# Layer 2 of a four-layer model on one core: a buffer for every gathered pair of rows, the first half's gathers issued during the second half's routing, and GpSimd's instructions in written order

## The chip, the cores and the metric

The kernel runs on one core of a Trainium2 chip. The metric is the device time of one launch in microseconds (us). The engines are called as in the profile: PE is TensorE's matmul (PEld its weight loads), DVE is VectorE, ACT is ScalarE, POOL is GpSimd and SP is SyncE, which here only issues DMAs. POOL issues DMAs too, among them the indirect ones that gather rows by a list of indices.

## The reference

Four layers work on 4 x 512 = 2,048 tokens of 256 numbers in float32. Each layer normalizes the tokens and adds an attention part and a feed-forward part to them:

```python
xn = _layernorm(x, axis=-1)
x = x + _L2_attn_ref(xn, ...) + _L2_ffn_ref(xn, ...)
```

Layer 2 is the one that is changed. Its attention part mixes the heads inside each token:

```python
q = (x @ Wq.T + bq).reshape(b, l, h, hd)
kv = (x @ Wkv.T + bkv).reshape(b, l, 2, hd)
k, v = (kv[:, :, 0], kv[:, :, 1])
attn = jnp.einsum('blhd,bld->blh', q, k)[..., None] / math.sqrt(hd)
attn = jax.nn.softmax(attn, axis=-1)
out = (attn * v[:, :, None, :]).reshape(b, l, -1)
```

Its feed-forward part sends each token to 2 of 8 small experts, and all tokens through one shared gated unit:

```python
scores = jax.nn.softmax(jnp.einsum('th,eh->te', xf, gate_w), axis=-1)
topk_w, topk_i = jax.lax.top_k(scores, K)                 # K = 2 of E = 8
topk_w = topk_w / jnp.sum(topk_w, axis=-1, keepdims=True)
cw = jnp.zeros_like(scores).at[jnp.arange(T)[:, None], topk_i].add(topk_w)
g = jnp.einsum('th,ehi->eti', xf, wg)
u = jnp.einsum('th,ehi->eti', xf, wu)
eo = jnp.einsum('eti,eih->eth', jax.nn.silu(g) * u, wd)
y = jnp.einsum('te,eth->th', cw, eo)
shared = jax.nn.silu(xf @ sg) * (xf @ su) @ sd
return (y + shared).reshape(b, s, h)
```

## The kernel before

The 2,048 tokens lie as 16 tiles of 128 rows; the running sum x stays in on-chip memory, and xnT holds the normalized tokens turned. Layer 2 treats the tokens in two halves of 8 tiles. For each half:

- `Half.dispatch` routes: `router` (L1199) computes the scores, and the rest counts how many tokens each expert gets and gives each chosen (token, expert) pair a slot in a list sorted by expert. The list has up to 23 tiles of 128 slots, `PAIRS` groups them into 11 pairs of tiles and a last single one. The result is `ids` (L1342), which row of the normalized tokens belongs in each slot, and `expert`, which expert each tile uses.
- `Half.gather` (L1367 to L1376) fetches the rows: one indirect DMA per tile, issued by POOL, from a copy of the normalized tokens in DRAM into a buffer `xs` that holds one pair.
- `Half.experts` runs the pairs through PE in a short pipeline: `turn` transposes the gathered rows (L1390, copied by ACT at L1395), `hidden` multiplies by the gate and up weights (L1402), ACT applies Silu (L1409) and DVE multiplies (L1410), `turn_hidden` transposes that (L1416, L1418), and `down` multiplies by the down weights (L1424), which DVE copies to `os` (L1429) and SP writes to DRAM (L1431).
- `Half.combine` gathers each token's two results (L1468, POOL) and adds them to x with their weights on DVE (L152).

`head_mix` (L1148) is the attention part, one sequence of four tiles at a time: PE projects (L142), DVE adds the bias into `qkv` (L1160), DVE and ACT compute the softmax `s` (L1165 to L1176), POOL multiplies it with v (`prod`, L1177) and DVE adds that to x (L1182). `qkv` and `prod` have one buffer each.

`weave` takes several such generators and writes their pieces one after another, always from the one that is the least far along in its share. `Layer2.run` calls it three times: the shared unit with the routing of both halves; then the experts of the first half with the mixer and the gathers of the second half; then the experts of the second half with the combining of the first. The gathers of the first half are pulled by its `experts`: two pairs at the start and one in each step of its loop, into three buffers (`xs0`); the second half has twelve buffers of its own (`xs1`).

What the program writes is not yet the order of an engine's instructions. The framework draws that order when the program is complete: it models the time of each instruction and lets an engine take the earliest written one of those that are ready by the model; waits for buffers count as well. Each engine then runs its list strictly in that order. `keep_in_program_order` ties an instruction behind the one that was written before it for the same engine.

Pools of buffers are stacked from two ends of on-chip memory. A pool takes the space of earlier ones once these are closed, and its first use then waits for the last reader of what it overlaps. Layer 2's pools are opened from the right: `t_rows`, `t_xs` (the gathered rows), `t_temp` (the experts' temporaries) and `h_t` (the mixer's and the shared unit's, called the mixer's pool here).

Of the kernel before, what the change touches and what calls it, by code (L numbers as in the profile page):

```python
# [15 lines left out]
P = 128  # L16
NB, SEQ, DM = 4, 512, 256
# [65 lines left out]
def v3(ap, b):  # L83
    return ap.rearrange("p (a b) -> p a b", b=b)
# [54 lines left out]
def project_tokens(c, out, w, cols, tokens):  # L139

    for d in range(2):
        c.nc.tensor.matmul(  # L142
            out, lhsT=c.xnT[:, d, tokens], rhs=w[:, d, cols], start=(d == 0), stop=(d == 1)
        )
# [69 lines left out]
def weave(c, *streams, flush=True):  # L214

    live = [[start * total, total, gen] for gen, total, start in streams]
    while live:
        s = min(live, key=lambda s: s[0] / s[1])  # L220
        cost = next(s[2], None)
        if cost is None:
            live.remove(s)
        else:
            s[0] += cost
        c.step()
    if flush:
        c.step(True)
# [644 lines left out]
def product_key_pieces(c, a, keep, pool, dram, xn):  # L873
# [110 lines left out]
    for k in range(K):  # L984
        gather(0, k)
# [162 lines left out]
def head_mix(c, pool, w, b):  # L1148

    nc = c.nc  # L1150
    H, HD, W = 16, 16, 288
    wqkv = v3(w[:, : 2 * W], W)
    bias = w[:, 2 * W : 3 * W]
    qkv = c.tile(pool, [P, TPB, W], "qkv")
    c.settle(b)
    for t in range(TPB):
        tt = b * TPB + t
        pq = c.ps()[:, :W]
        project_tokens(c, pq, wqkv, slice(0, W), slice(tt * P, (tt + 1) * P))
        nc.vector.tensor_add(qkv[:, t, :], pq, bias)  # L1160
        yield 0.5
    full = [P, TPB, H, HD]
    prod = c.tile(pool, full, "prod")
    heads = lambda v: v.rearrange("p t (h d) -> p t h d", d=HD)
    nc.vector.tensor_mul(  # L1165
        prod, heads(qkv[:, :, :256]), qkv[:, :, 256:272][:, :, None, :].to_broadcast(full)
    )
    s = c.tile(pool, [P, TPB, H], "s", bufs=2)
    nc.vector.tensor_reduce(s, prod, AX.X, ALU.add)

    top = c.tile(pool, [P, TPB, H], "top", bufs=2)
    nc.vector.tensor_copy(top, s)
    nc.vector.tensor_sub(s, s, top)
    nc.scalar.activation(s, s, AF.Exp, scale=HD ** -0.5)
    nc.vector.reciprocal(top, s)
    nc.vector.tensor_mul(s, s, top)  # L1176
    nc.gpsimd.tensor_mul(  # L1177
        prod, s[:, :, :, None].to_broadcast(full),
        qkv[:, :, 272:288][:, :, None, :].to_broadcast(full),
    )  # L1180
    x = c.x[:, b * TPB : (b + 1) * TPB, :]
    nc.vector.tensor_add(x, x, prod.rearrange("p t h d -> p t (h d)"))  # L1182
    c.part_done(b)
    yield 1.0
# [45 lines left out]
PAIRS = [[t for t in (2 * j, 2 * j + 1) if t < NS] for j in range((NS + 1) // 2)]  # L1230
# [3 lines left out]
class Half:  # L1234
# [129 lines left out]
        nc.vector.tensor_mul(w, w, tot[:, None, :].to_broadcast([P, 2, HT]))  # L1364
        yield 1.0

    def gather(self, pool, bufs, js):  # L1367

        for j in js:
            x = self.xs[j] = self.c.tile(pool, [P, 2, DM], f"xs{self.hf}", bufs=bufs)  # L1370
            for i, t in enumerate(PAIRS[j]):
                self.c.nc.gpsimd.indirect_dma_start(
                    out=x[:, i, :], out_offset=None, in_=self.xn,
                    in_offset=bass.IndirectOffsetOnAxis(ap=self.ids[:, t : t + 1], axis=0),
                )
            yield 1.0  # L1376

    def experts(self, weights, pool, opool, more):


        c, nc = self.c, self.c.nc
        pairs, xs = PAIRS, self.xs
        xsT, hs, hT = {}, {}, {}

        def turn(j):
            pt = c.ps("tr")
            n = len(pairs[j])
            for i in range(n):
                for d in range(2):
                    nc.tensor.transpose(  # L1390
                        pt[:, (2 * i + d) * P : (2 * i + d + 1) * P],
                        xs[j][:, i, d * P : (d + 1) * P], c.ident,
                    )
            xsT[j] = c.tile(pool, [P, 4, P], "xsT", bufs=2)
            nc.scalar.copy(xsT[j][:, : 2 * n, :], v3(pt[:, : 2 * n * P], P))  # L1395

        def hidden(j):
            ph = v3(c.ps(), 2 * P)
            n = len(pairs[j])
            for i, t in enumerate(pairs[j]):  # L1400
                for d in range(2):
                    nc.tensor.matmul(  # L1402
                        ph[:, i, :], lhsT=xsT[j][:, 2 * i + d, :],
                        rhs=weights[:, bass.ds(where[t] + 2 * d * P, 2 * P)],
                        start=(d == 0), stop=(d == 1),
                    )
            sg = c.tile(pool, [P, 2, P], "gate", bufs=2)
            hs[j] = c.tile(pool, [P, 2, P], "hs", bufs=2)
            nc.scalar.activation(sg[:, :n, :], ph[:, :n, :P], AF.Silu)  # L1409
            nc.vector.tensor_mul(hs[j][:, :n, :], sg[:, :n, :], ph[:, :n, P:])  # L1410

        def turn_hidden(j):
            pt = c.ps("tr")
            n = len(pairs[j])
            for i in range(n):
                nc.tensor.transpose(pt[:, i * P : (i + 1) * P], hs[j][:, i, :], c.ident)  # L1416
            hT[j] = c.tile(pool, [P, 2, P], "hsT", bufs=2)
            nc.scalar.copy(hT[j][:, :n, :], v3(pt[:, : n * P], P))  # L1418

        def down(j):  # L1420
            po = v3(c.ps("acc"), DM)
            n = len(pairs[j])
            for i, t in enumerate(pairs[j]):
                nc.tensor.matmul(  # L1424
                    po[:, i, :], lhsT=hT[j][:, i, :],
                    rhs=weights[:, bass.ds(where[t] + 4 * P, DM)], start=True, stop=True,
                )
            os = c.tile(opool, [P, 2, DM], "os", bufs=2)
            nc.vector.tensor_copy(os[:, :n, :], po[:, :n, :])  # L1429
            rows = self.out[2 * j * P : (2 * j + n) * P, :]  # L1430
            nc.sync.dma_start(rows.rearrange("(i p) d -> p i d", p=P), os[:, :n, :])  # L1431

        where = []
        N = len(pairs)
        if more:
            next(more)
            next(more)
        for lo in (0, 12):
            where.extend(nc.values_load_multi_w_load_instructions(
                self.expert[:1, lo : min(lo + 12, NS)], engines=[mybir.EngineType.PE],  # L1440
                min_val=0, max_val=(E8 - 1) * EW,
                skip_runtime_bounds_check_because="the chip has limited them to the last expert's",
            )[1])
        turn(0)
        yield 0.5
        for j in range(N + 2):
            if more:
                next(more, None)
            if j < N:
                hidden(j)  # L1450
                yield 1.7
            if j + 1 < N:
                turn(j + 1)
            if j >= 2:
                down(j - 2)
                yield 0.9
            if 1 <= j <= N:
                turn_hidden(j - 1)
            yield 0.6
# [22 lines left out]
class Layer2:  # L1482
# [24 lines left out]
    def run(self):  # L1507
        c, a = self.c, self.a
        self.rows = self.pool("t_rows")
        with ExitStack() as stack:  # L1510
            xs, temp, mixer = (self.pool(name, stack) for name in ("t_xs", "t_temp", "h_t"))
            unit = c.unit(a["t_shared"])
            h_small = c.tile(mixer, [P, 864], "h_small")
            c.nc.sync.dma_start(h_small, a["h_unit"])

            def dispatch():
                for half in self.halves:
                    yield from half.dispatch()

            def mix():  # L1520
                for b in range(NB):
                    yield from head_mix(c, mixer, h_small, b)

            shared = glu_pieces(c, mixer, [unit], n=2, width=256, loaded=True, bufs=4)
            first, last = self.halves
            every = range(len(PAIRS))
            experts = [
                half.experts(self.weights, temp, self.rows, more)
                for half, more in ((first, first.gather(xs, 3, every)), (last, None))
            ]  # L1530
            weave(c, (shared, 41.0, 0.0), (dispatch(), 34.0, 0.0), flush=False)
            weave(
                c, (experts[0], 40.0, 0.0), (mix(), 12.0, 0.0),
                (last.gather(xs, len(PAIRS), every), 12.0, 0.0), flush=False,
            )
            weave(c, (experts[1], 40.0, 0.0), (first.combine(self.rows), 11.0, 0.2), flush=False)

# [232 lines left out]
```

## Time and profile before

| | us |
|---|---|
| runs of the kernel | 3228.06, 3241.74, 3240.93; median 3240.93 |
| profiled execution | 3211.92, of it span 3210.0 |
| PE busy | 3093.7 (96% of the span) |
| DVE busy | 1858.1 (58%) |
| ACT busy | 1262.3 (39%) |
| POOL busy | 653.1 (20%) |
| mean granted TensorE clock | 0.991 |

Layer 2 lies between about 1576 and 1755 us of the span. The 46 gathers of both halves are 46 instructions of L1372 on POOL between 1601.3 and 1686.3 us, with a median of 0.949 us each; from their issue to the landing of the rows it takes 2.7 to 7.1 us, with a median of 3.4. Layer 3 fills the time from 1755 on, with PE busy nearly throughout.

A row of a timeline gives start, duration, engine, line, operation, output and inputs, and in brackets how long the engine had been idle and what ended that. The table by stage gives busy time of each engine in a stretch; PEclk in it is the part of its full clock that PE was granted.

### The profile page before, as it was taken

How to read it: one execution, taken by the hardware profiler on the slowest of the kernel's cores; microseconds unless marked ns; L12 is line 12 of the kernel's file. 1: busy time of each engine (PE TensorE's matmuls, PEld its weight loads, DVE VectorE, ACT ScalarE, POOL GpSimd, SP SyncE). 2: the span in 40 equal slices, each digit the busy share in tenths (PEclk: the TensorE clock that was granted, in tenths of full speed). 3: DMA queues.
4: the chain of work that ended last, by engine and by line, in shares of the span. 5: the costliest groups of instructions: out<-in, count | busy, mean ns of one | idle time of the engine just before them, and what ended most of it. 6: DMA issues, size and time to landing. Idle time of an engine off the chain costs nothing.

```text
span 3210.0 us, 35838 instructions
## 1 busy us (share of the span) xinstructions
PE 3093.7 (96%) x12502; PEld 1888.0 (59%) x12502; DVE 1858.1 (58%) x4730; ACT 1262.3 (39%) x2910; POOL 653.1 (20%) x525
## 2 busy tenths in 40 slices
PE   8999999998899999999989999999999999999999
PEld 5566556565555555555567565665665665555555
DVE  4778778887677677768656655545545522222222
ACT  4434444443455666657525433333333411111111
POOL 0464546556300122322053100000000000000000
PEclk9999999999999999999999999999999999999999
DMA  3232323332311144344133000000000000000000
GB/s 122 83 107 94 122 89 105 101 96 80 98 35 35 42 118 110 97 102 136 57 102 118 15 1 27 1 27 1 7 14 1 20 20 20 20 20 20 0 0 27
DMA packets 88947, 183.59 MB, mean 57 GB/s; under 512 B 14176, under 2 KB 57200, under 8 KB 84160
## 3 DMA queue, kind: packets, MB, share of 16 engines
q1 hardware_dynamic: 74304, 133.48, 13.0%
q0 software_dynamic: 14176, 47.01, 5.9%
q8 instruction: 99, 1.62, 0.2%
q10 hardware_dynamic: 288, 0.82, 0.1%
q14 instruction: 80, 0.66, 0.1%
HBM read 159.38 MB, written 12.98 MB: 54 GB/s over the span
## 4 chain that ended last, share of the span: by engine, by line
PE 74%; DVE 12%; DMA 5%; POOL 4%; ACT 3%; issue 2%; SPq 1%; DVEq 0%; ACTq 0%; POOLq 0%
PE mm L134 28%; PE acc L203 8%; PE mm L627 8%; PE mm L142 5%; PE acc L1091 4%; PE acc L643 3%; DMA G<-own 3%; DVE cy L268 2%; DVE G L409 2%; PE tr L1083 2%; PE tr L806 2%; PE acc L850 2%; PE acc L863 2%; POOL y L458 1%; DMA psw<-pes 1%
## 5 line engine op out<-in xcount | busy, mean ns | idle before, releaser
L134 PE MATMUL mm<-xnT,wu 128*128 128x512 f32 x2128 | 958.5, 597 | 7.4 <-ACT sg L388 2.9
L134 PEld LDWEIGHTS mm<-xnT,wu 128*128 128x128 f32 x2128 | 400.4, 191 | 461.2 <-issue 432.6
L634 ACT ACTIVATE pr<-pr,nm 128x128 f32<-128x128 f32 (+3 forms) x512 | 285.9, 559 | 305.3 <-DVE nm L630 302.7
L195 ACT ACTIVATE sg<-mm 128x512 f32<-128x512 f32 x168 | 99.9, 595 | 604.8 <-PE mm L134 604.6
L196 DVE TENSOR_TENSOR hT<-sg,mm 128x512 f32<-128x512 f32 x168 | 115.1, 685 | 383.3 <-PE mm L134 372.8
L203 PE MATMUL acc<-wu,hT 128*128 128x256 f32 x1344 | 304.8, 380 | 0.6 <-DVE hT L196 0.5
L630 DVE CUSTOM_DVE_ANT_0 pr<-mm,late 128x128 f32<-128x128 f32 (+3 forms) x512 | 244.8, 483 | 83.4 <-PE mm L627 78.6
L203 PEld LDWEIGHTS acc<-wu,hT 128*128 128x128 f32 x1344 | 252.2, 190 | 53.6 <-issue 20.4
L134 PE MATMUL mm<-xnT,w_in 128*128 128x512 f32 x512 | 232.7, 598 | 7.2 <-DVE cy L268 5.1
L967 POOL DMA_INDIRECT e<-in_p_experts,ids x128 | 128.3, 1002 | 494.2 <-DVE x L152 463.2
L409 DVE TENSOR_TENSOR_SCAN G<-G,eye 128x1024 f32<-128x1024 f32 x64 | 156.7, 2448 | 55.9 <-DMA G<-own 55.8
L627 PE MATMUL mm<-kf,qf 128*128 128x128 f32 (+3 forms) x512 | 176.8, 445 | 8.9 <-DVE qf L785 6.4
L435 POOL TENSOR_TENSOR G<-G,CB 128x1024 f32<-128x1024 f32 x64 | 151.2, 2363 | 149.0 <-ACT CB L361 79.7
L627 PE MATMUL mm<-k,q 128*128 128x128 f32 (+3 forms) x512 | 176.6, 435 | 1.1 <-DVE q L1056 1.1
L268 DVE SCALAR_TENSOR_TENSOR cy<-mm,ws,cy 128x509 f32<-128x509 f32 (+2 forms) x216 | 158.5, 741 | 29.8 <-ACT cy L264 26.4
L421 ACT ACTIVATE xD<-xc,ws 128x128 f32<-128x128 f32 x256 | 84.3, 390 | 203.0 <-POOL y L458 197.1
L134 PEld LDWEIGHTS mm<-xnT,w_in 128*128 128x128 f32 x512 | 97.2, 192 | 112.4 <-issue 97.8
L152 DVE SCALAR_TENSOR_TENSOR x<-acc,cw,x 128x256 f32<-128x256 f32 x128 | 61.9, 484 | 155.6 <-PE acc L203 155.6
L1091 PE MATMUL acc<-PT,V 128*128 128x512 f32 (+3 forms) x512 | 149.5, 433 | 0.0
L151 DVE TENSOR_TENSOR x<-acc,x 128x256 f32<-128x256 f32 x176 | 74.0, 422 | 129.0 <-PE acc L643 98.3
L1056 DVE TENSOR_SCALAR q<-mm,bias 128x512 f32<-128x512 f32 x64 | 48.0, 750 | 169.1 <-PE mm L134 169.1
L495 PE MATMUL tr<-wo,y 128*128 128x256 f32 x512 | 128.8, 395 | 9.1 <-DVE x L151 3.5
(306 smaller groups left out, 4977.2 us busy)
## 6 DMA issues: line engine op xcount, KB each, us to landing
G<-own SPq DMA_DIRECT2D x64, 512.0 KB, 4.2
w_in<-in_m_units SPq DMA_DIRECT2D x16, 1024.0 KB, 5.0
eb<-since SPq DMA_DIRECT2D x96, 128.0 KB, 3.4
wu<-in_o_units SPq DMA_DIRECT2D x8, 1536.0 KB, 6.6
wo<-in_m_units SPq DMA_DIRECT2D x16, 512.0 KB, 4.2
psw<-pes SPq DMA_DIRECT2D x128, 64.0 KB, 2.5
wu<-in_f_units SPq DMA_DIRECT2D x4, 1536.0 KB, 7.1
wu<-in_l_units SPq DMA_DIRECT2D x4, 1408.0 KB, 9.6
```

The costliest lines, as they stand in the source:

```text
L134: c.nc.tensor.matmul(out, lhsT=w[:, d, cols], rhs=c.xnT[:, d, tokens], start=(d == 0), stop=(d == 1))
L142: c.nc.tensor.matmul(out, lhsT=c.xnT[:, d, tokens], rhs=w[:, d, cols], start=(d == 0), stop=(d == 1))
L203: nc.tensor.matmul(po, lhsT=hT[k][:, t * P : (t + 1) * P], rhs=wd[:, k, :], start=(i == 0), stop=(i == per - 1),)
L268: nc.vector.scalar_tensor_tensor(y[:, j:], src[:, : SEQ - j], conv[:, k, 3 - j : 4 - j], y[:, j:], ALU.mult, ALU.add,)
L409: nc.vector.tensor_tensor_scan(flat, flat, eye.rearrange("p h t -> p (h t)"), 0.0, ALU.mult, ALU.add)
L435: nc.gpsimd.tensor_mul(G, G, seqs[b][2][:, t, :][:, None, :].to_broadcast([P, HG, P]))
L495: nc.tensor.matmul(po, lhsT=y[:, k, :], rhs=groups[i][1][:, k, :], start=(k == 0), stop=(k == 3))
L627: nc.tensor.matmul(sc, lhsT=q[:, i * P : n], rhs=k[:, :n], start=True, stop=True)
L630: nc.vector.tensor_tensor_reduce(out=pr, in0=sc, in1=late[:, SEQ - n :], scale=1.0, scalar=-NEG, op0=ALU.add, op1=ALU.min, accum_out=nm,)
L634: nc.scalar.activation(pr, pr, AF.Exp, bias=nm, scale=-1.0, accum_out=total)
L967: nc.gpsimd.indirect_dma_start(out=e, out_offset=None, in_=a["p_experts"], in_offset=bass.IndirectOffsetOnAxis(ap=ids[:, t, k : k + 1], ax ...
L1091: nc.tensor.matmul(z[:, j * P :], lhsT=head["V"][:, j, h, :], rhs=head["PT"][:, j, j * P :], start=(j == 0), stop=(j == TPB - 1),)
```

## The change

The change touches the gathers of layer 2, their buffers and one multiplication.

- `gather` no longer has a number of buffers and a list of pairs as arguments. Both halves use one tag, `xs`, with 24 buffers, one for each pair of both halves.
- The gathers of the first half are written between the pieces of the second half's routing, one pair a piece, instead of being pulled by the first half's `experts`; the argument `more` and its calls go.
- The gathers of both halves, and the mixer's multiplication on POOL, are tied into the order in which they are written.
- In the second weave the share of the second half's gathers is counted as 16 instead of 12.

```diff
-    nc.gpsimd.tensor_mul(
+    c.tc.keep_in_program_order(nc.gpsimd.tensor_mul(
         prod, s[:, :, :, None].to_broadcast(full),
         qkv[:, :, 272:288][:, :, None, :].to_broadcast(full),
-    )
+    ))
...
-    def gather(self, pool, bufs, js):
-
-        for j in js:
-            x = self.xs[j] = self.c.tile(pool, [P, 2, DM], f"xs{self.hf}", bufs=bufs)
-            for i, t in enumerate(PAIRS[j]):
-                self.c.nc.gpsimd.indirect_dma_start(
+    def gather(self, pool):
+
+        for j, pair in enumerate(PAIRS):
+            x = self.xs[j] = self.c.tile(pool, [P, 2, DM], "xs", bufs=2 * len(PAIRS))
+            for i, t in enumerate(pair):
+                self.c.tc.keep_in_program_order(self.c.nc.gpsimd.indirect_dma_start(
                     out=x[:, i, :], out_offset=None, in_=self.xn,
                     in_offset=bass.IndirectOffsetOnAxis(ap=self.ids[:, t : t + 1], axis=0),
-                )
+                ))
             yield 1.0
...
-    def experts(self, weights, pool, opool, more):
+    def experts(self, weights, pool, opool):
...
-        if more:
-            next(more)
-            next(more)
...
-            if more:
-                next(more, None)
...
+            first, last = self.halves
+
             def dispatch():
-                for half in self.halves:
-                    yield from half.dispatch()
+                yield from first.dispatch()
+                rows = first.gather(xs)
+                for piece in last.dispatch():
+                    next(rows, None)
+                    yield piece
+                yield from rows
...
-            first, last = self.halves
-            every = range(len(PAIRS))
-            experts = [
-                half.experts(self.weights, temp, self.rows, more)
-                for half, more in ((first, first.gather(xs, 3, every)), (last, None))
-            ]
+            experts = [half.experts(self.weights, temp, self.rows) for half in self.halves]
             weave(c, (shared, 41.0, 0.0), (dispatch(), 34.0, 0.0), flush=False)
             weave(
-                c, (experts[0], 40.0, 0.0), (mix(), 12.0, 0.0),
-                (last.gather(xs, len(PAIRS), every), 12.0, 0.0), flush=False,
+                c, (experts[0], 40.0, 0.0), (mix(), 12.0, 0.0), (last.gather(xs), 16.0, 0.0),
+                flush=False,
             )
```

## The prediction

> **What bounds the kernel now.** I read four views, from coarse to fine. The share of busy time and the busy slices come first: TensorE (PE) is busy 96% of the span, so only a stretch in which it is not busy can give time back. The table by stage of layer 2 (columns: stretch, its length, busy time and count on PE, PEld, DVE, ACT, POOL, then the granted TensorE clock, the DMA share, GB/s) finds one:
>
> ```profile
> 1591.30:1612.60 21.30, 21.27 (x104) 14.76 (x104) 11.96 (x44) 4.53 (x7) 5.79 (x6) 1.00 0.16 38
> 1615.10:1639.60 24.50, 24.10 (x105) 15.94 (x105) 15.33 (x61) 2.38 (x4) 8.87 (x10) 1.00 0.16 44
> 1639.60:1652.50 12.90, 12.64 (x61) 10.30 (x61) 6.26 (x12) 4.86 (x10) 10.16 (x10) 1.00 0.71 221
> 1652.50:1664.10 11.60, 0.03 (x1) 0.06 (x1) 0.78 (x2) 1.91 (x3) 8.62 (x10) 0.62 0.54 127
> 1664.10:1668.70 4.60, 4.60 (x12) 3.30 (x13) 1.02 (x2) 0.59 (x1) 3.62 (x4) 0.50 0.43 103
> 1668.70:1705.00 36.30, 35.95 (x182) 30.06 (x180) 23.60 (x43) 15.43 (x31) 15.96 (x12) 1.00 0.36 93
> ```
>
> For 11.6 us PE does nothing, and for the 4.6 us after that it works at half its clock. The waits of that stretch name the cause: the transposes of a gathered pair (L1390) wait for its rows.
>
> ```profile
> PE tr L1390 <- DMA xs<-xn_half,ids: 11.6, 1, 11.6
> DVE x L1182 <- POOL prod L1177: 8.3, 3, 4.1
> ```
>
> Why the rows are late stands in POOL's timeline (start, duration, engine, line, operation; idle before and its releaser in brackets):
>
> ```profile
> 1601.29 1.00 POOL L1372 DMA_INDIRECT xs<-xn_half,ids  x1 [86.14 <-DVE ids L1342]
> ...
> 1607.65 0.95 POOL L1372 DMA_INDIRECT xs<-xn_half,ids  x1 [0.30 <-issue]
> 1622.26 1.01 POOL L1372 DMA_INDIRECT xs<-xn_half,ids  x1 [13.66 <-PE tr L1390]
> 1623.58 1.00 POOL L1372 DMA_INDIRECT xs<-xn_half,ids  x1 [0.30 <-issue]
> 1630.62 0.95 POOL L1372 DMA_INDIRECT xs<-xn_half,ids  x1 [6.04 <-DVE tot L1363]
> ...
> 1660.41 0.94 POOL L1372 DMA_INDIRECT xs<-xn_half,ids  x1 [0.30 <-issue]
> ...
> 1670.13 1.95 POOL L1177 TENSOR_TENSOR prod<-s,qkv 128x1024 f32<-128x1024 f32 x1
> ```
>
> Six gathers fill the first half's three buffers. Two more follow when a buffer is read. Then, from 1630.62, when the second half's indices are there, come its 23 gathers in one run: the 24th and 25th issue from 1630.62, at 1659.15 and 1660.41, are pair 4 of the first half, and the chain of waits gives the last of them 3.53 us to land, at 1663.9. Pair 4 was needed at 1652.5. So the stall is an order on POOL, forced by three buffers.
>
> **The change, part by part.**
>
> *Buffers and the earlier gathers.* All 23 gathers of the first half can be issued from 1601.29, one every 1.25 us (0.95 of issue and 0.30 of idle): 23 x 1.254 = 28.8, so the last leaves at about 1630 and lands by 1634 (3.4 us median). The second half's indices come at 1630.34, so its gathers don't move later for it. Pair 4 lands near 1617 for a need at 1652.5. The wait of 11.6 us goes. What ends last in its place: ACT still has the Exp and its table loads, with the gate of pair 3 ending at 1654.43 and the copy of pair 4 (0.59) after that, so pair 4's first product starts at about 1655.1 where it started at 1669.07. PE fills the gap with the down product (0.86) and a mixer product (0.97). That is 14.0 us: 11.6 of wait, and of the slow stretch 2.3 (4.6 at clock 0.50 does what 2.3 at 1.00 does), with 0.1 from reading starts.
>
> The clock: the rows show 0.50 for 4.6 us after an empty 11.6. The Trainium skill (TensorE: Matmul & The Clock Gate, "What's actually happening") gives the slow time after an idle window as about 3.4 us, so an estimate by that page returns 1.7 us and not 2.3, and the sum would be 0.6 smaller; the measured row decides.
>
> *The mixer's product on GpSimd (L1177), now in written order.* In trace order it stands behind three pairs of the second half's gathers, then four, four and one pair between the others (progress 2/12, 5/12, 8/12, 11/12 of the mixer's stream against j/16 of the gathers' stream). The six gathers end near 1638; the product waits for s on DVE, ready at 1653.59; so it runs at 1653.6 and not at 1670.13. Queued behind it on POOL are the other gathers of the second half; who waits for those is the second half's experts, whose transposes start at 1706.0 now and 1692 then. Eight gathers (10.0) and one product (1.95) make 12.0 us between two products, against the 13.0 to 13.9 by which they follow each other now (1670.13, 1684.05, 1697.68, 1710.72). So gathers end before each product is due; the last row is asked for after the third product, at about 1683, and lands at 1686.5. Cost on PE: 0, hidden by that slack of 1 us or more a sequence. If the cover goes, DVE's add (L1182) waits; today it waits up to 4.1 us with PE at work. I keep 0 to 5 for the range.
>
> A rule speaks against gathering beside routing. The rows: the eight gathers issued beside routing took 0.95 to 1.01 us, with DVE busy 11.96 of 21.3; beside the mixer's wide DVE products some took up to 1.93. The Trainium skill (SBUF — State Buffer, "SBUF: two separate sides") holds that descriptor writing for a DMA from GpSimd is locked out while VectorE runs an instruction in a two-port mode, and gives 3.1 us for one of 0.62. By that, as an estimate, 23 gathers cost 23 x 2.5 = 57 us more, POOL is free only at 1687, and the kernel gets slower by tens of us; the rows of this routing show none of it, and I go by them.
>
> *More space.* The pool of rows grows from 15 to 24 tiles of 2,048 bytes, so what is opened after it (t_temp, h_t) lies 18,432 bytes lower. Today the load of h_small starts at 1580.80 and ACT's first Silu of the shared GLU waits 3.92 us, both until layer 1's last L863 ends (1580.73): the mixer's pool overlaps buffers that L863 reads. Lower down it lies in layer 1's other pool, free when L850 ends (1576.23). So that Silu can start up to 3.1 us earlier. Bounds: 0 to 3.1 gained, but DVE is busy 15.91 of 16.70 us between 1574.6 and 1591.3, so only about 0.8 of it can move, and I take 0.4. The lower mixer also reaches into layer 3's first pool: its bias load (SP, 1576.29) and mask (DVE, 0.38 and 0.21) then wait for the mixer's end, near 1700. On SP the bias load then stands between the writes of expert rows (L1431). First read: 1757.4. Cost 0, hidden by those 57 us; without them, about 3.3 (the landing of h_small's load).
>
> *Pulled pairs.* The calls by which the experts pulled gathers issue nothing else; the same 46 DMAs move the same bytes. Cost 0. Layer 3, 1,455 us with PE busy nearly throughout, keeps its instructions.
>
> **Sum:** 14.0 + 0.4 = 14.4 us less. The profiled execution took 3211.92 (span 3210.0 and 1.9 around it), so 3197.5 on its own scale. The median of the runs is 3240.93, which is 29.0 more and not explained by the trace; I carry the difference over: 3226.5.
>
> **Rivals.**
> - *More goes than the stall* (0.20). Other PE gaps of layer 2 are 1.16 (for ACT's Silu), 0.78, 0.82, 2.5 (1612.6 to 1615.1) and 1.05 us, and the order is drawn anew. For: buffers no longer hold transposes back. Against: most wait for DVE chains that stay. All of it: 6.3 more, 3220; at best.
> - *Half is taken back* (0.11). A new wait of 5 us at the first products, since pair 4 now meets the Exp's table loads (1.28 each) and the late add of the mixer: 9 gained, 3231.5. For: ACT ran the gate of pair 3 at 1654.05, after PE had already stopped. Against: the same loads at 1681.51 and 1695.14 cost PE nothing.
> - *It doesn't do what it says* (0.05): rows come early but the products stay behind something else, 3241. Against: only the rows' arrival ended that wait.
> - *Slower* (0.16): POOL becomes the pace in the mixer stage. If gathers run at the slow 1.93 + 0.30 = 2.23, the first half's end at 1652.6, six of the second at 1666.0, and the first product is 12.4 late; with 4.1 of slack, PE loses 8.3. Each of the next two products comes 8 x 2.23 + 2.0 = 19.8 after the last, against 13.8: 6.0 each. With three restarts at half clock, 2.3 each: 8.3 + 12.0 + 6.9 = 27.2 lost, 12.8 net, 3254. It decides from a pitch of (13.8 - 2.0) / 8 = 1.47 us a gather. For: 1.93 was seen beside wide DVE work. Against: 42 of the 46 issues took 0.94 to 1.01.
>
> **The numbers.** The forecast, 14.4 less, gets 0.48; its own range is 3218 to 3234 (the 5 us of the mixer's wait one way, and half of the other gaps the other, with some scatter of the runs, which spread over 13.7). 0.5% of 3240.93 is 16.2 us, about what a measurement of this kernel can tell from no change, so the line is at 3224.7, close to the forecast: I split its chance evenly, 0.24 and 0.24. Faster: 0.24 + 0.20 = 0.44. The slower case splits 0.08 and 0.08. Within: 0.24 + 0.11 + 0.05 + 0.08 = 0.48. Slower: 0.08. The range, 3207 to 3243, holds the forecast, the gaps of the first rival with the scatter of the runs, the half and the no-change case; the slower case is left out.
>
> **What would show it.** Right: 23 gathers in one run from about 1601 to 1630; no wait of L1390 for xs; clock 1.00 from 1640 to 1700; first L1177 near 1654 and the transposes of the second half near 1692; the start of layer 3's products 14 us earlier. Wrong: L1372 above 1.47 us on average; POOL ending a wait of L1182 that PE then shares; a new empty PE stretch between 1640 and 1700, or a longer stretch after 1755.

## The result, and the profile after

The changed kernel took 3240.51 us in the median of 20 runs (3225.73 to 3253.59). The kernel before, run beside it, took 3241.38 (3228.06 to 3251.29, 20 runs). The ratio is 0.9996 with a 95% interval of 0.9983 to 1.001: no difference that can be measured. The profiled execution took 3236.5 us, with a span of 3234.7. The profiled execution of the kernel before, on which the forecast was built, was shorter than all 20 of its runs: 3211.92. What that means turned out to be the heart of the case.

What the change was to do inside layer 2, it did. GpSimd's timeline (start, duration, engine, line; idle before and its releaser in brackets) has the 23 gathers of the first half in one run, the second half's right behind its routing, and the mixer's product (L1177) in its written place:

```profile
1612.39 1.00 POOL L1372 DMA_INDIRECT xs<-xn_half,ids  x1 [89.41 <-DVE ids L1342]
1613.70 0.98 POOL L1372 DMA_INDIRECT xs<-xn_half,ids  x1 [0.30 <-issue]
...
1640.10 0.95 POOL L1372 DMA_INDIRECT xs<-xn_half,ids  x1 [0.30 <-issue]
1660.70 0.95 POOL L1372 DMA_INDIRECT xs<-xn_half,ids  x1 [19.65 <-DVE tot L1363]
...
1683.40 1.92 POOL L1177 TENSOR_TENSOR prod<-s,qkv 128x1024 f32<-128x1024 f32 x1 [15.49 <-DVE s L1176]
```

No transpose of L1390 waits for rows any more. But the table by stage of the changed kernel (same columns as in the prediction) has new empty stretches of TensorE, of 4.8, 12.1 and 5.6 us, all of them in the routing:

```profile
1594.90:1599.70 4.80, 0.08 (x2) 0.06 (x1) 4.71 (x26) 0.73 (x2) 0.00 (x0) 0.88 0.16 54
1599.70:1623.60 23.90, 23.89 (x104) 16.21 (x104) 9.67 (x36) 4.22 (x6) 8.63 (x9) 0.88 0.18 45
1623.60:1635.70 12.10, 0.00 (x0) 0.03 (x1) 3.89 (x15) 1.88 (x2) 9.20 (x10) 0.59 0.38 103
1635.70:1642.90 7.20, 7.19 (x20) 4.23 (x20) 1.23 (x8) 0.00 (x0) 4.12 (x5) 0.74 0.53 85
1642.90:1648.50 5.60, 0.12 (x2) 0.05 (x1) 3.49 (x18) 0.60 (x1) 0.00 (x0) 0.80 0.18 19
```

During the 12.1 us VectorE is busy for 3.89 and ScalarE for 1.88, so neither of them is the limit. The waits of this stretch name a releaser that is not in the profile ("remote"):

```profile
ACT sg L195 <- remote: 15.1, 1, 15.1
...
DVE hT L196 <- remote: 8.0, 1, 8.0
DVE total L1285 <- remote: 7.7, 1, 7.7
```

In order of time, the same place reads:

```profile
1620.00 3.60 PE L134 MATMUL mm<-xnT,wu 128*128 128x512 f32 x8
...
1627.99 1.28 ACT L195 ACT_TABLE_LOAD   x1 [4.45 <-remote]
...
1633.65 0.69 DVE L196 TENSOR_TENSOR hT<-sg,mm 128x512 f32<-128x512 f32 x1 [8.01 <-remote]
...
1635.71 0.66 PE L1279 MATMUL mm<-chosen,con 128*128 128x64 f32 x2 [12.11 <-issue]
```

The eight products of L134 are recorded as finished at 1623.6. ScalarE needs the first four (done at 1621.9) and starts at 1628.0. VectorE needs the last four and starts at 1633.65, ten microseconds late. TensorE's next product waits for VectorE. So what is late is not a product but the news of it: the count that TensorE raises when a group of products is done. I call such a completion late when the trace has no update of that count within 0.25 us of the group's end. In this execution 147 of 3,056 are late, nearly all of them in runs of five or more GpSimd gathers or just behind one, in layers 1 and 2 alike. Some of them have no record at all (2,984 updates of the count are recorded), but the starts of the other engines show that the news itself came late. The updates recorded at 1622.31, 1627.92 and 1633.56 are 5.6 us apart; ScalarE starts 0.07 us behind the second of them and VectorE 0.09 us behind the third. Behind the last gathers, five more come between 1644.78 and 1644.99. In the profiled execution of before that the forecast rests on, 4 were.

### The profile page after: what moved, and what is told of

It reads as the page before. It is cut to its first block, busy times and chain, and to the rows that moved or that the text cites. A ratio compares the mean times of both kernels' runs of the same rounds, so it can differ in the third digit from the quotient of the medians.

```text
span 3234.7 us, 35838 instructions
## 1 busy us (share of the span) xinstructions
PE 3102.3 (96%) x12502; PEld 1889.5 (58%) x12502; DVE 1862.9 (58%) x4730; ACT 1261.6 (39%) x2910; POOL 649.0 (20%) x525
## 4 chain that ended last, share of the span: by engine, by line
PE 76%; DVE 12%; DMA 4%; POOL 3%; ACT 3%; issue 2%; another core or an unknown queue 0%; SPq 0%; DVEq 0%; ACTq 0%; POOLq 0%
PE mm L134 29%; PE acc L203 9%; PE mm L627 8%; PE mm L142 5%; PE acc L1091 4%; PE acc L643 3%; DMA G<-own 3%; DVE cy L268 2%; DVE G L409 2%; PE tr L1083 2%; PE tr L806 2%; PE acc L850 2%; PE acc L863 2%; PE mm L1402 1%; PE tr L495 1%
## 5 line engine op out<-in xcount | busy, mean ns | idle before, releaser
L134 PE MATMUL mm<-xnT,wu 128*128 128x512 f32 x2128 | 959.0, 597 | 7.1 <-ACT sg L388 2.9
L134 PEld LDWEIGHTS mm<-xnT,wu 128*128 128x128 f32 x2128 | 400.4, 191 | 460.9 <-issue 433.4
L134 PE MATMUL mm<-xnT,w_in 128*128 128x512 f32 x512 | 231.5, 596 | 6.7 <-DVE cy L268 5.1
L967 POOL DMA_INDIRECT e<-in_p_experts,ids x128 | 128.1, 1001 | 508.4 <-DVE x L152 474.1
L134 PEld LDWEIGHTS mm<-xnT,w_in 128*128 128x128 f32 x512 | 96.4, 191 | 111.1 <-issue 96.7
L806 PEld LDWEIGHTS tr<-con,pr 128*128 128x128 f32 x640 | 81.1, 143 | 97.6 <-ACT pr L799 35.9
```

The source lines that it names most:

```text
L134: c.nc.tensor.matmul(out, lhsT=w[:, d, cols], rhs=c.xnT[:, d, tokens], start=(d == 0), stop=(d == 1))
L806: nc.tensor.transpose(pt[:, (i - j) * P : (i - j + 1) * P], prs[s][i][:, j * P : (j + 1) * P], c.ident)
L967: nc.gpsimd.indirect_dma_start(out=e, out_offset=None, in_=a["p_experts"], in_offset=bass.IndirectOffsetOnAxis(ap=ids[:, t, k : k + 1], ax ...
```

## The experiments

The times in one table. Kernels of one set ran on one chip, beside the kernel before; "layer 2" is from the end of its last L863 to the end of its last L1424 in the profiled execution (for the kernel before: 168.0 in the first profile). Between executions of one kind it varies by 0.1 to 0.3 us for the changed kernel and the one before (by 2.3 for paced), while the time up to its start varies by up to 16 between the executions of one kind.

| set | kernel | median us | before us | ratio (95%) | layer 2 us | late |
|---|---|---|---|---|---|---|
| result | changed | 3240.51 | 3241.38 | 0.9996 (0.9983–1.0010) | 184.7 | 147 |
| 1 | before_again | 3238.70 (1 run) | 3247.42 | | 183.2 | 140 |
| 1 | after_again | 3241.56 (1 run) | 3247.42 | | 184.4 | 160 |
| 1 | none_beside | 3246.57 | 3247.42 | 0.9997 (0.9980–1.0014) | 184.3 | 147 |
| 1 | six_beside | 3246.65 | 3247.42 | 1.0002 (0.9988–1.0016) | 184.4 | 155 |
| 2 | paced | 3213.48 | 3211.89 | 1.0006 (0.9996–1.0015) | 166.7 | 5 |
| 2 | twice | 3263.33 | 3211.89 | 1.0155 (1.0138–1.0171) | 218.9 | 2 |
| 2 | plain | 3206.69 | 3211.89 | 0.9986 (0.9975–0.9996) | 163.0 | 5 |
| 2 | gated | 3219.36 | 3211.89 | 1.0028 (1.0013–1.0042) | 176.2 | 4 |
| 3 | before_c | 3203.52 (1 run) | 3207.96 | | 168.1 | 2 |
| 3 | after_c | 3195.46 | 3207.96 | 0.9959 (0.9946–0.9973) | 159.1 | 2 |
| 3 | paced_c | 3208.50 | 3207.96 | 1.0004 (0.9992–1.0016) | 169.0 | 2 |
| 3 | split | 3201.67 | 3207.96 | 0.9977 (0.9966–0.9989) | 162.7 | 2 |
| 4 | paced_d | 3236.98 | 3250.10 | 0.9971 (0.9953–0.9989) | 177.5 | 152 |
| 4 | plain_d | 3228.05 | 3250.10 | 0.9942 (0.9922–0.9963) | 169.4 | 129 |
| 5 | flight2 | 3212.61 | 3213.04 | 0.9997 (0.9984–1.0010) | 170.2 | 4 |
| 5 | flight3 | 3200.57 | 3213.04 | 0.9970 (0.9955–0.9985) | 157.1 | 4 |
| 6 | flight3_e | 3234.20 | 3246.05 | 0.9965 (0.9945–0.9985) | 183.4 | 156 |
| 7 | space | 3248.52 | 3244.32 | 1.0007 (0.9991–1.0023) | 186.7 | 148 |

The last column splits the sets into two kinds, with nothing between: the kernel before takes 3241 to 3250 us where completions are late and 3208 to 3213 where they come on time. Of the sets 1 to 7, those with late completions came from three chips (4 and 6 from the same one), those with completions on time from three others. What a kernel gains is read within a kind only.

**Is it the change, or the execution?** Both kernels, unchanged, once more.

> The kernel before, unchanged, one more profiled execution. Theory A (gathers in one run beside the routing hold back TensorE's completions): layer 2 from its last L863 to its end is again near 179 us, with the 11.6 us wait of L1390 and no wait longer than 3 us of ACT or DVE for a TensorE product that the trace shows as done. Rival B (the two profiled executions differ by chance, the whole kernel apart): an execution of typical length, near 3240 us, shows such late completions here too, and layer 2 is nearer 195 us.

> The changed kernel, one more profiled execution. Theory A: the late completions (ACT's and DVE's waits of 4 to 15 us near the run of 23 gathers) are there again, layer 2 near 195 us. Rival B: they lie elsewhere or are gone, and layer 2 is near 165 us, 14 shorter than before's 179.

The kernel before has late completions as well (140), and so the claim that only the change brings them fell at once. Its layer 2 is 183.2 us here and not 168, and the stall that I had seen is of another kind:

```profile
ACT gate L1409 <- remote: 23.4, 1, 23.4
...
PE mm L1402 <- ACT xsT L1395: 20.7, 1, 20.7
```

TensorE is empty for 20.7 us after 1656.8, where the profile I predicted from had 11.6. The transposes before it had their rows and are recorded as done at 1656.8; ScalarE's copy of them starts at 1676.8. GpSimd's run of 23 gathers lasts here from 1644.3 to 1672.7. So where completions are late, the stall of the kernel before was not a wait for rows alone, and having the rows earlier need not end it.

**Moving the gathers in the text, without moving them.** Two kernels were to take gathers away from the routing:

```diff
 # none_beside
-                for piece in last.dispatch():
-                    next(rows, None)
-                    yield piece
+                yield from last.dispatch()
 # six_beside
-                for piece in last.dispatch():
-                    next(rows, None)
+                for i, piece in enumerate(last.dispatch()):
+                    if i < 3:
+                        next(rows, None)
```

> The changed kernel with every gather of the first half moved behind the second half's routing (still 24 buffers, written order). Theory A: no late completion beside the routing; the first products wait some 5 us for rows, so 3240.5 - 17 + 5, near 3229 us. Rival B: no difference from the changed kernel but for that wait, near 3245 us.

> The changed kernel with only six gathers (three pairs) beside the second half's routing, as the kernel before has them, and the other 17 of the first half behind it, ahead of the second half's. Pair 4 is asked for ahead of the second half's rows, so the 11.6 us wait of L1390 should be gone. Theory A: late completions gone or few, near 3226 us (the forecast of the whole change). Rival B: same as the changed kernel, near 3240 us.

Both miss: layer 2 takes 184.3 and 184.4 us, and GpSimd's timeline still has 23 gathers in a row, in none_beside from 1622.6 to 1651.3, beside the routing. The edit changed when the gathers are written down relative to other engines' work, but GpSimd has nothing else to do then, and a gather starts as soon as its row numbers are there. The two runs test nothing about the gathers' place; they are two more executions of the changed kernel. They give one thing: in none_beside the updates of TensorE's count are recorded at 1645.98, 1651.58, and then five between 1655.09 and 1655.27. The trace has the last five groups of products before that end between 1650.6 and 1654.8, over 4.2 us, so their completions were held and then let go together, when the landings of the last gathers were counted too (1655.2 to 1655.6).

**Four edits to tell apart gathers, their rate, their traffic and the new order.** In short:

```diff
 # paced: in gather(), behind each indirect_dma_start of the first half
+                for _ in range(2 - 2 * self.hf):
+                    self.c.tc.keep_in_program_order(self.c.nc.gpsimd.tensor_copy(
+                        self.c.tile(pool, [P, 4, P], "pace"), <identity, broadcast>))
 # twice: each gather of the first half issued two times
-            for i, t in enumerate(pair):
+            for i, t in [(i, t) for i, t in enumerate(pair) for _ in range(2 - self.hf)]:
 # plain: a load in place of the gather
+                self.c.nc.sync.dma_start(
+                    x[:, i, :], self.xn[t % HT * P : (t % HT + 1) * P, :])
 # gated: first.gather(xs) behind both dispatches, and ahead of it
+                c.tc.keep_in_program_order(c.nc.gpsimd.tensor_copy(
+                    c.tile(xs, [P, NS], "gate", U32), last.ids))
```

> The changed kernel with two small copies on GpSimd behind each gather of the first half (128x512 each), so that the 23 gathers no longer follow each other at 1.25 us but at some 2.4, from about 1617 to 1672. Theory A (a run of back-to-back gathers holds back TensorE's completions until its last rows land; beside the routing this costs 14.4 + 2.9 us of empty TensorE): late completions in the routing gone, layer 2 some 15 us shorter, 3241 - 15 = 3226 us. Rival C (the gaps of 4.7, 14.4 and 2.9 come from the new order of instructions on VectorE and TensorE, whatever GpSimd does): gaps stay, 3241 us.

> The changed kernel with each gather of the first half issued twice into the same place, so 46 in the first run instead of 23, 57 us long instead of 29. Theory A: TensorE's completions stay late until about 1678, some 20 to 28 us more of empty TensorE, 3262 to 3269 us. Rival C: only the rows come later, pair j at twice its time, still ahead of the transposes that read them; 3241 us.

> The changed kernel with the 46 indirect gathers replaced by plain loads of as many rows of the same table, issued by SyncE; it leaves the choice of the rows out, so the output is not the reference's. Theory A: no late completion in layer 2 before the combine, empty TensorE of layer 2 falls from 30 to about 10 us, 3241 - 20 = 3221 us. Rival D (it is the traffic of rows as such, 6 MB, that holds completions back, whichever queue asks for it): late completions stay with the loads, 3235 to 3241 us. Rival C: 3241 us.

> The changed kernel with a GpSimd instruction ahead of the first half's first gather that reads the second half's row numbers, so that all 46 gathers lie behind the second half's routing. Theory A: no late completion between 1617 and 1640, the routing's gaps of 14.4 and 2.9 us go; the late ones appear beside the first half's products instead, from about 1645 to 1673, as in the kernel before (20.7 us of empty TensorE there); 3240 to 3250 us. Rival C: the gaps in the routing stay and the wait for rows comes on top, 3255 us or more.

This set met a chip where completions come on time (the kernel before: 3211.89), so the late ones could not be removed, and none of the four says anything on them. What it says is the price of the written order on GpSimd. In twice, the 46 gathers of the first half and six of the second stand ahead of the mixer's first product, and each repeated gather waits for the landing of the first, so what stands ahead of the product lasts until 1726. VectorE's waits and TensorE's:

```profile
DVE x L1182 <- POOL prod L1177: 38.4, 4, 30.8
...
PE mm L1402 <- DVE qkv L1160: 36.9, 3, 33.2
```

VectorE stands 30.8 us at its add (L1182) for the product, behind the add stands L1160, which adds the bias to TensorE's products and so frees the buffer that they lie in, and TensorE stands 33.2 us for that. In gated the same chain costs 9.7 us, and in split (below) 3.4. So the 3263 us of twice is the figure that theory A named, for another reason: a number that fits is no proof of the cause.

**The change where completions are on time.** The kernels before and after once more, paced again, and one that gates only 17 of the gathers:

```diff
 # split
-                for piece in last.dispatch():
-                    next(rows, None)
-                    yield piece
+                for i, piece in enumerate(last.dispatch()):
+                    if i < 3:
+                        next(rows)
+                    yield piece
+                <the gate of gated>
                 yield from rows
```

> The kernel before, unchanged, for its trace beside the other three. Theory A says that a set of executions is of one kind: if this one is near 3212 us, no completion of TensorE is late anywhere and L1390 waits 11.6 us for rows; if it is near 3241, over 100 completions are late, all of them in runs of gathers.

> The changed kernel, unchanged. Theory A (the change removes the wait for rows, and only completions held back by its run of 23 gathers take the gain away): where the kernel before is near 3212 us, this one is 14 less, 3198; where it is near 3241, the same as it. Rival C (the new order of instructions in the routing costs what the stall gave, hold or not): no difference in either case; 3212 beside 3212.

> The changed kernel with GpSimd's gathers of the first half spread to 2.4 us or more apart, again. Beside a kernel before near 3212 us it took 3213.5. Theory A: beside a kernel before near 3241 us it has no late completion in the routing and takes 3226; rival C: 3241.

> The changed kernel with six gathers of the first half ahead of, and the other 17 held behind, the second half's row numbers by a GpSimd instruction that reads them: the rows of pair 4 are then asked for third and fourth after the routing instead of 24th and 25th. Theory A: no stall for rows, no run of gathers in the routing. Beside a kernel before near 3212 us: 3198; beside one near 3241: the late completions lie beside the first half's products, 3235 to 3245. Rival C: 3212 and 3241.

Here the change does what was forecast: ratio 0.9959 (0.9946 to 0.9973), 12.5 us by the medians. Layer 2 falls from 168.1 to 159.1. TensorE's waits in it, of the kernel before first:

```profile
PE tr L1390 <- DMA xs<-xn_half,ids: 11.5, 1, 11.5
PE mm L1279 <- DVE chosen L1264: 2.5, 1, 2.5
...
PE mm L1279 <- ACT sg L195: 1.2, 1, 1.2
...
PE mm L1336 <- DVE at L1329: 0.8, 1, 0.8
PE tr L121 <- DVE xn L110: 0.8, 1, 0.8
```

and of the changed kernel:

```profile
PE mm L1336 <- DVE at L1329: 4.7, 1, 4.7
PE mm L1279 <- DVE chosen L1264: 2.5, 1, 2.5
```

The wait for rows is gone and no other took its place there; the 4.7 us at L1329 are new, and come up again below. Rival C, that the new order in itself costs what the stall gave, falls. Split has the change's buffers and written order, but only six gathers beside the routing, as the kernel before has; that it is 0.23% faster than before shows that asking for pair 4's rows third and fourth behind the routing, not 24th and 25th, gives part of the gain. Paced costs 13 us against the changed kernel (3208.50 beside 3195.46), and one reason shows: its copies and the gathers behind them keep GpSimd from the mixer's product, for which VectorE waits 12.4 us in all.

**Spread gathers and plain loads where completions are late.** The same two kernels, on a chip of the other kind:

> The changed kernel with the first half's gathers spread, once more, to meet an execution with late completions (kernel before near 3241 or above). There, theory A (a run of back-to-back gathers holds the completions back): none late in the routing; layer 1's and the second half's runs still cost their part, so some 10 us less than the kernel before. Rival F (any gather does it, however far apart): late ones all along its 57 us, 5 to 15 us more than the kernel before. Where the kernel before is near 3210: no difference, as twice measured.

> The changed kernel with plain loads in place of the 46 gathers (which rows is left out, so the output is not the reference's), once more for the same reason. Where the kernel before is near 3241 or above: theory A, no late completion in layer 2 before the combine, and 20 us less than the kernel before; rival D (the traffic of rows as such), late ones beside the loads, within 5 us of it. Where the kernel before is near 3210: 5 us less, as measured.

This set decides which gathers bring the late completions. With the first half's gathers 2.4 us or more apart,

```profile
1619.69 1.00 POOL L1372 DMA_INDIRECT xs<-xn_half,ids  x1 [89.11 <-DVE ids L1342]
1620.70 1.30 POOL L1377 COPY pace<-con 128x512 f32<-128x512 f32 x2
1622.15 0.99 POOL L1372 DMA_INDIRECT xs<-xn_half,ids  x1
```

no completion is late from 1544 to 1652, though 152 are late elsewhere in the same execution. TensorE's two longest waits in the stretch are about those that the same kernel has where completions are on time (5.3 and 4.4 us in paced_c):

```profile
PE mm L1336 <- DVE at L1329: 5.1, 3, 4.7
PE mm L1279 <- DVE chosen L1264: 4.4, 1, 4.4
```

Beside the rest of the spread gathers three completions are late, by 1.0 us at most. The other 28 of layer 2 come behind 1678, when the second half's gathers and then those of the combining run at 1.25 us again. The empty stretches of 12 to 14 us are gone, layer 2 takes 177.5 us where the changed kernel took 184.3 to 184.7, and the kernel is 0.29% faster than before (0.11 to 0.47) although the copies themselves cost time. So it is gathers that follow each other at 1.25 us, and not gathers as such (rival F). With plain loads, which move as many bytes on SyncE's queue, no completion is late from 1546 to 1728, layer 2 takes 169.4, and the kernel is 0.58% faster (0.37 to 0.78). The loads wait for no row numbers and so run earlier, from 1599.1 to 1617.2, but 27 groups of products end in that time and none of them is late; so it is not the traffic of the rows (rival D). TensorE's longest waits from there to 1740 are short (L1401 is L1402 of the kernel before):

```profile
PE mm L1336 <- DVE at L1329: 4.6, 2, 2.4
PE mm L1401 <- issue: 3.3, 1, 3.3
PE mm L1279 <- DVE chosen L1264: 2.5, 1, 2.5
```

**A limit on the gathers under way.** Ahead of each gather, GpSimd reads one column of a row block asked for u gathers earlier, in both halves:

```diff
+                if t >= u:
+                    self.c.tc.keep_in_program_order(self.c.nc.gpsimd.tensor_copy(
+                        self.c.tile(pool, [P, 1], "seen"), asked[t - u]))
                 <the gather>
+                asked.append(x[:, i, :1])
```

> The changed kernel with a one-column GpSimd copy ahead of each gather, in both halves, that reads a row block asked for two gathers earlier: no more than two gathers are under way, and a late landing puts off the next one. Theory A with the backlog in the handling of landings (rows land 2.4 us after their issue, yet the counts come late): the run slows to some 1.8 us a gather, and no completion is late by more than a few us. Beside a kernel before near 3210 us: 10 less; beside one near 3241 or above: 12 to 18 less. If the pitch of 1.25 was not what mattered: like the changed kernel, 12 less beside 3210, equal beside 3241.

> The same with three gathers under way: at 1.25 us a gather and 3.4 to land that hardly slows them where completions are on time, so 12 less beside a kernel before near 3210 us. Beside one near 3241 or above the backlog is bounded at three gathers: some late completions, 5 to 15 us less.

> The changed kernel with three gathers under way at most, once more, to meet an execution with late completions. Beside a kernel before near 3241 us or above: if their backlog is what holds TensorE's completions, the run of gathers slows by itself, the empty TensorE of the routing falls from 14.4 to below 6, and it is 5 to 15 us faster than the kernel before; if not, equal to it. Beside a kernel before near 3210 us: 10 to 12 less, as measured.

With u = 2 the run slows to 1.9 us a gather and the gain is lost, again to waits for L1160 (8.7 in all). With u = 3 it is faster than before on both kinds of chip, by 0.30% (0.15 to 0.45) and 0.35% (0.15 to 0.55). Where completions are on time it has the shortest layer 2 of all kernels that gather, 157.1. Where they are late only part of the expectation held: TensorE's empty stretches beside the routing, 14.4 and 2.9 us in after_again, are 3.8 and 5.2 here. But the run of gathers did not slow by itself (1.40 us a gather, where flight3 has 1.44), 16 completions there are still late, the clock stays at half for 23.9 us from 1644.1, and layer 2 of the profiled execution (183.4) is hardly shorter than that of the changed kernel. That execution was the slowest of nine (3246.4, of 3222.9 to 3246.4), so the gain of the runs stands without a trace that shows where it comes from.

**The lower pool alone.** One empty stretch, 4.7 us at L1329, is in every variant that has the change's layout and gathers, on both kinds of chip (with plain loads there are two waits at that place, 4.6 us in all):

```diff
 # space: the kernel before, with
+            c.nc.gpsimd.memset(c.tile(xs, [P, 9 * 2 * DM], "spare")[:, :1], 0.0)
```

> The kernel before with a spare tile of 18,432 bytes in the pool of rows, and nothing else of the change: the shared GLU's pool then lies as low as in the changed kernel. The empty TensorE of 4.7 us at VectorE's L1329, seen in every variant of the changed kernel and not in the kernel before. If it comes from the lower pool (earlier h_small, first Silu and first products of the shared GLU, so TensorE runs out of work earlier): it is here too, in place of three gaps of 1.2, 0.8 and 0.8, and the stall for rows stays; layer 2 from its last L863 to its last L1424 about 2 us longer than before, 170 beside 168.1 (or 185 beside 183.2, where completions are late). If it comes from the gathers or GpSimd's written order: gaps as before, 168 (or 183).

```profile
PE mm L1336 <- DVE at L1329: 4.7, 1, 4.7
PE mm L1279 <- DVE chosen L1264: 3.6, 1, 3.6
```

It is there, with nothing of the gathers or of GpSimd's order changed, and the gaps of 1.2, 0.8 and 0.8 are not. So it comes from the place of the pool. The runs can't tell the two kernels apart (1.0007, 0.9991 to 1.0023); layer 2 is 3.5 us longer than in before_again, in one trace each.

## Why the prediction was wrong

*The step that failed* is the last of the sum: "The median of the runs is 3240.93, which is 29.0 more and not explained by the trace; I carry the difference over: 3226.5." It takes the 29 us for something that lies elsewhere and stays. It does not. Between before_again and before_c the spans differ by 35.2 us: 4.4 lie ahead of layer 1's first gather (L967), where the two kinds do not differ (836 to 849 us in ten of the traces), 15.1 from there to the end of the last L863, in the stretch with layer 1's runs of up to eight gathers, 15.1 in layer 2, and 0.6 behind it. The trace on which every term was costed was of a kind in which completions come on time; the runs that the forecast was held to were of the other kind. There the change moves a run of 23 gathers from beside the products to beside the routing, a chain in which VectorE and TensorE wait for each other at each step, and the late completions cost 25.3 us of layer 2 (159.1 to 184.4) where they cost the kernel before 15.1 (168.1 to 183.2). The gain of 9.0 in layer 2 becomes a loss of 1.2. Where completions come on time the change gains 12.5 us in the runs (8.7 to 17.3 by the interval) and 9.0 in layer 2 of the traces, against the 14.4 of the forecast.

*The wait for rows (11.6)*: right in cause and, where completions are on time, in size. TensorE's empty time in layer 2 falls from 19.72 us (before_c) to 9.65 (after_c), by 10.1.

*The slow clock (2.3)*: the stretch at half clock after the stall went, but it came back elsewhere. After the new empty 4.7 us the changed kernel was at 0.50 for 10.2 us from 1585.8, and 3.4 more from 1616.5 (after_c). So TensorE's busy time did not fall but rose by 1.1 us (148.38 to 149.45 over layer 2), and 10.1 - 1.1 = 9.0 is what layer 2 gained.

*More space (0.4 gained)*: wrong in sign. The first Silu did start earlier, 2.5 us ahead of the end of the last L863 in after_c and 1.4 us behind it in before_c. What followed was one wait of 4.7 us at VectorE's L1329 instead of three that sum to 2.8, long enough for the clock to fall. That TensorE had done the shared unit's products earlier and had none left for this place is my reading; space shows only that the lower pool brings the wait.

*The mixer's product in written order (0, with 0 to 5 kept)*: right where the gathers keep their pitch; VectorE's wait for it was 5.0 us in three waits in after_c's stretch to 1700, with TensorE at work. The rival "slower" named the right chain: L1177, L1182, and behind that L1160 and TensorE. In twice, gated, split and paced gathers late on GpSimd made it decide.

*The terms put at 0 behind layer 2*: right. From its end to the end of the program both kernels take 1461.3 us (before_c and after_c).

*Gathers beside routing*: the issue times were right, 0.94 to 1.19 us in after_c, and of the 57 us that the rule on descriptor writing (the Trainium skill, SBUF — State Buffer, "SBUF: two separate sides") would have added there is no sign. What no row of that profile could show is that such gathers, at 1.25 us each, can hold back another engine's completions. The rival that I did weigh, GpSimd's pace, was the wrong price for the right place.

*The warning that was there*: the profiled execution lay 16 us below the fastest of the three runs shown. I carried the difference over without asking what it was made of. That the measured 3240.51 lies inside the stated range is luck: the range was drawn to hold the case of no change, and the rival that named 3241 (chance 0.05) had no late completion in its reason.

## What to carry to other kernels

Before costing a change, see whether the profiled execution belongs to the runs that it will be judged by. If it lies outside them, another trace comes first, since a difference that is "not explained" may lie exactly where the change works. Work that only fills an idle engine can still be dear: where completions are late, a run of back-to-back gathers cost more beside work that needs an answer from TensorE at each step (25.3 us of layer 2) than beside the products (15.1). A limit of three under way cost nothing measurable here. An order written out for one engine is safe only as long as everything ahead in it is on time.

## What was not expected of the hardware

On three chips, TensorE's completions came late during runs of GpSimd gathers at 1.25 us each, by up to 20 us (before_again); on three others 2 to 5 of some 3,050 were late, by 2 us at most. The rows themselves were not late: the packets of the first half's gathers ended 2.3 to 5.1 us after the issue in after_again, and 2.3 to 4.6 in after_c. In none_beside and in the result the last five held completions came within some 0.2 us of each other. The traces of the late kind also hold fewer records of semaphore updates, that is, of counts raised (18,071 for the changed kernel, where after_c has 20,623), and 1,589 of the 2,552 missing are landings on the gathers' own counts. Whether the recording takes part in holding completions back stays open, since every execution here was recorded, and so does the rate at which it begins: at 1.4 us a gather (flight3_e) completions were still late, at 2.4 (paced_d) not. Sets 4 and 6 met the same chip and were of the same kind, which speaks for a property of the chip; it wasn't tried further.

In layer 2 of these traces every stretch at half clock lasts a multiple of 3.41 us, and the gap of 4.7 us brought 6.8 (flight3) to 10.2 us (after_c) at half clock, of which 5.1 and 7.7 lie behind the gap, while one of 2.5 us was followed by none (before_c) or by 3.4 us (after_c). The Trainium skill (TensorE: Matmul & The Clock Gate, "What's actually happening") gives some 3.4 us of slow time after an idle window; these rows show one and a half to over two times that.
